# Attention steps in turns of two, in a fused two-layer kernel on one core

## The chip, the core and the metric

The kernel runs on one core of one Trainium2 chip. Its metric is the device time of one execution in microseconds, median of several. The engines are named as the profile names them: PE (TensorE matmul) with PEld (its weight loads), DVE (VectorE), ACT (ScalarE), POOL (GpSimd) and SP (SyncE, which here only issues transfers).

## What is computed

x has 8 sequences (batches) of 512 tokens and 256 channels, in float32. Two blocks follow each other, with 16 heads of 16 channels:

```python
x = x + _L0_attn_ref(_layernorm(x), Wqkv_w, Wqkv_b, conv_w, conv_b, out_w, out_b)
x = x + _L0_ffn_ref(_layernorm(x), wq, wk, wv, wo, w_router, wg, wu, wd, g1, g2)
```

The first: q, k, v; causal attention (a1); a convolution of three taps over its context, whose output is the q of a second causal attention (a2) on the same k and v; the output projection. The second: RMS norm, q and k rotated by position, causal attention (a3), output projection and residual; RMS norm, a router that picks 2 of 8 experts for each token, and the experts' gated units of 704. So there are three attentions for each of 8 batches.

## The kernel before, in words

`block_kernel` runs `fast_path`, and `general_path` after it only if counters at its end say so; with these inputs it doesn't run. All that follows is in `fast_path`.

**Attention.** `attention(qT, kT, v, to)` (L1100 on) is a generator for one of the 24 attentions. Keys are taken in blocks of 64 (NB = 8); a step takes one or two of them, so that each step has 512 columns of queries, and an attention has 9 steps (STEPS): four for the first 128 channels (`ch` 0), one that both halves share (the block `mid`), four for the second. A step does the following.

- Scores: on PE (L1188), 4 heads at a time in tiles of 32 rows, into two PSUM tiles `sc` of two banks each, for half of the heads each. The pool `ps_sc` has two buffers, so the next step writes the same two.
- Exponentials: on ACT (L1195), one for each half, from `sc` to the SBUF tile `pr` (four buffers).
- The mask of the diagonal blocks: on POOL (L1205).
- Values: `times_v` on PE (L1121) in tiles of 64 rows by 32 columns, into two banks `av`. It is put off: `behind` holds the functions of two steps, and `catch_up` runs the oldest.
- When a half's last block is in (`last`), `normalise` copies both `av` banks to `cs` on ACT (L1138), and SP moves their parts across partitions (`r<-cs`, then `cs<-cs`, L1146 and L1147). Two functions follow some steps later: `finish` on DVE (reciprocal and product in two halves, L1152 and L1153), and `check` on ACT (a sum for the counters, L1156).

**Units.** All other work of attention's stage is cut into units, which are methods of `Batch`:

- of a1: `stats`, `normed`, `transpose(d)`, `k(ch)`, `q(ch)`, `values(half)`
- between a1 and a2: `conv(ch, first, n)`, n of 6 terms of two channel halves and three taps; it keeps its bank until the last one
- between a2 and a3: `bias`, `x1(half)`, `stats2`, `transpose2(d)`, `k2(ch)`, `q2(ch)`, `values2(half)`, `normed2(c)`. `rotate` copies a projection on ACT, and its `rotation` follows on DVE; `split` then writes both halves of kT on ACT
- after a3: `h(half)`, `rms`, `transpose3(d)`, `route`, `slots`. `slots` puts eight transfers of rows to the experts' table into `to_send`, which `send` issues on POOL one by one.

Most units write a PSUM tile by `mm_tile`, which hands out two banks in turn, so a third unit needs the first one's bank emptied, by ACT or DVE.

**Order.** PE, ACT, DVE and POOL execute in the order in which the program emits (`manual_schedule`); SP isn't bound to it. Batches go in pairs, one in each lane. The order of attentions is a1 of both, a2 of both, a3 of both. Each step emits scores, values of the step two before, the mask, the functions due in `due[False]`, its units, those due in `due[True]`, and one `send`:

```python
                for step in range(STEPS):
                    next(steps)
                    next(steps)
                    next(steps)
                    follow_up(end=False)
                    beside(n, step)
                    follow_up()
                    send()
```

The units stand in tables by attention and step: `first_lane` and `second_lane` (a1's inputs of a coming batch), `between`, `middle` and `end`. Ahead of the first step stand all of batch 0's units, and batch 1's up to its transposes. `fill` writes a piece of the experts' table with padding by SP, one with each of the first 24 steps.

**Experts.** The last part (`expert_tile` and the loop over `places`) starts when attention ends; its first tile is begun among the last steps.

Of the kernel before, what the change touches and what calls it, by code (L numbers as in the profile page):

```python
# [18 lines left out]
P = 128  # L19
# [604 lines left out]
def fast_path(  # L624
# [28 lines left out]
    STEPS = DC * NB // 2 + 1  # L653

# [190 lines left out]
    with ExitStack() as att:  # L845
# [150 lines left out]
        def rotary_table(to, of):  # L996
            ps = mm_tile()
            for c in range(NC):
                t = small.tile([P, P], F32, tag="rope", name="rope", bufs=2)
                for a in range(2):  # L1000
                    nc.vector.tensor_copy(
                        t.rearrange("p (h a f) -> p h a f", a=2, f=HD // 2)[:, :, a],
                        of[a][:, c].unsqueeze(1).to_broadcast(halves),
                    )
                nc.tensor.transpose(ps[:, c * P : (c + 1) * P], t, ident)
            nc.scalar.copy(to, ps)

        def tables(n):
            if n == 0:
                nc.vector.tensor_scalar_mul(nsin_sb, sin_sb, -1.0)  # L1010
                rotary_table(cosT, (cos_sb, cos_sb))
            else:
                rotary_table(sinT, (nsin_sb, sin_sb))
# [74 lines left out]
        def catch_up():  # L1088
            for f in behind.pop(0):
                f()  # L1090


        due = {True: [], False: []}

        def follow(steps, f, end=True):
            due[end].append([steps, f])

        def follow_up(end=True):
            ready = [f for n, f in due[end] if n == 0]
            due[end][:] = [[n - 1, f] for n, f in due[end] if n]  # L1100
            for f in ready:
                f()

        def attention(qT, kT, v, to):

# [25 lines left out]
            def normalise(ch):  # L1131
# [26 lines left out]
                follow(2 - ch, finish)  # L1158
                follow(5 - 2 * ch, check, end=False)
# [21 lines left out]
            for parts in steps:  # L1181
# [14 lines left out]
                yield  # L1196
                if len(behind) == 2:
                    catch_up()
                behind.append([lambda parts=parts, pr=pr: values(parts, pr)])
                yield  # L1200
# [29 lines left out]
        class Batch:  # L1230
# [29 lines left out]
            def transposed(self, d, to, of, scale=None):  # L1260
# [5 lines left out]
                if scale is None:  # L1266
                    nc.scalar.copy(to[:, d, :S], ps)
                else:
# [149 lines left out]
            def transpose2(self, d):  # L1418
                if d == 0:
                    self.xaT = self.tile([P, DC, S], "xT", "xaT")  # L1420
                self.transposed(d, self.xaT, self.xa, g1_sb)

            def rotate(self, w, ch, to, later):
# [13 lines left out]
                follow(later - 1, rotation, end=False)  # L1437
                return t0

            def k2(self, ch, later=1):  # L1440
# [3 lines left out]
                t0 = self.rotate(wk_sb, ch, None, later)  # L1444
# [9 lines left out]
                follow(2 * later - 1, split)  # L1454

            def q2(self, ch, later=1):
                if ch == 0:
                    self.qT = self.q_tile("qT")
                self.rotate(wq_sb, ch, self.qT[:, ch, :], later)
# [123 lines left out]
        def first_lane(t):  # L1583

            return {
                (0, 4): [t.stats],
                (0, 6): [t.normed],
                (1, 0): [lambda: t.transpose(0)],
                (1, 1): [lambda: t.transpose(1)],
                (1, 2): [lambda: t.k(0)],  # L1590
                (1, 5): [lambda: t.q(0)],
                (2, 0): [lambda: t.values(0)],
                (2, 1): [lambda: t.values(1)],
                (2, 2): [lambda: t.k(1)],
                (2, 4): [lambda: t.q(1)],
            }

        def second_lane(t):

            return {  # L1600
                (0, 1): [t.stats],
                (0, 2): [t.normed],
                (0, 3): [lambda: t.transpose(0), lambda: t.transpose(1)],
                (1, 0): [lambda: t.k(0)],
                (1, 1): [lambda: t.q(0)],
                (1, 2): [lambda: t.values(0)],
                (1, 3): [lambda: t.values(1)],
                (1, 6): [lambda: t.k(1)],
                (2, 0): [lambda: t.q(1)],
            }  # L1610

        def conv_units(t, units):
            return {
                (0, step): [lambda ch=ch, first=first, n=n: t.conv(ch, first, n) for ch, first, n in fs]
                for step, fs in units.items()
            }

        def between(t):
            if t.lane == 0:
                units = {  # L1620
                    2: [(0, 0, 2)],
                    3: [(0, 2, 1), (1, 0, 1)],
                    4: [(1, 1, 2)],
                    5: [(0, 3, 2)],
                    6: [(0, 5, 1), (1, 3, 1)],
                    7: [(1, 4, 1)],
                    8: [(1, 5, 1)],
                }
            else:
                units = {  # L1630
                    1: [(0, 0, 2)],
                    3: [(0, 2, 2)],
                    4: [(0, 4, 2)],
                    5: [(1, 0, 1)],
                    6: [(1, 1, 2)],
                    7: [(1, 3, 2)],
                    8: [(1, 5, 1)],
                }
            units = conv_units(t, units)
# [52 lines left out]
        with tc.manual_schedule(  # L1692
# [8 lines left out]
            for fs in list(first.values())[2:]:  # L1701
                for f in fs:
                    f()
# [191 lines left out]
```

## Time and profile before

| | us |
|---|---|
| median of 3 runs | 1495.44 (1494.64 to 1496.28) |
| the profiled execution | 1502.59 |
| its span | 1500.7 |
| first scores to last values | 27.8 to 933 |
| first scores of pairs 0, 1, 2, 3 | 27.8, 256.8, 477.9, 700.7 |

The profiled execution's own time is 1.9 us over its span, and 7 us over the median of the runs. The profile is read by groups (a line of code, an engine, an operation), and by timelines, where a row has the start, the time, engine and line, tiles and shape, the number of instructions merged, and in brackets idle time before it with what ended it. A matmul in float32 stands in the trace as two passes, except transposes. Matmuls overlap and their ends are modelled, so what a burst of PE costs is read from its start to the next one's start.

### The profile page before, as it was taken

How to read it: one execution, taken by the hardware profiler on the slowest of the kernel's cores; microseconds unless marked ns; L12 is line 12 of the kernel's file. 1: busy time of each engine (PE TensorE's matmuls, PEld its weight loads, DVE VectorE, ACT ScalarE, POOL GpSimd, SP SyncE). 2: the span in 40 equal slices, each digit the busy share in tenths (PEclk: the TensorE clock that was granted, in tenths of full speed). 3: DMA queues.
4: the chain of work that ended last, by engine and by line, in shares of the span. 5: the costliest groups of instructions: out<-in, count | busy, mean ns of one | idle time of the engine just before them, and what ended most of it. 6: DMA issues, size and time to landing. Idle time of an engine off the chain costs nothing. (4 is left out here: it accounts for less than half of the span.)

```text
span 1500.7 us, 31797 instructions
## 1 busy us (share of the span) xinstructions
PE 1437.3 (96%) x13370; PEld 859.6 (57%) x13370; DVE 663.9 (44%) x1271; ACT 742.0 (49%) x1198; POOL 573.5 (38%) x615
## 2 busy tenths in 40 slices
PE   6799999999999999999999999999999999999995
PEld 3444555544555544555644545666676676676773
DVE  4153675663776653775643774422222222222221
ACT  3556788666788766788665885311112112112110
POOL 3333333563334563323563334443323323323322
PEclk9999999999999999999999998999999999999998
DMA  6920001210001210011211111242222313132300
GB/s 168 218 52 22 23 23 51 80 55 23 22 23 52 93 58 23 23 61 37 81 56 42 34 61 50 83 140 85 83 77 68 112 43 109 61 98 67 103 23 17
DMA packets 62841, 97.61 MB, mean 65 GB/s; under 512 B 13516, under 2 KB 39064, under 8 KB 62688
## 3 DMA queue, kind: packets, MB, share of 16 engines
q1 hardware_dynamic: 52608, 69.74, 15.6%
q0 software_dynamic: 10080, 25.74, 5.3%
q8 instruction: 107, 1.75, 0.5%
q14 instruction: 46, 0.38, 0.1%
HBM read 46.06 MB, written 32.61 MB: 52 GB/s over the span
## 5 line engine op out<-in xcount | busy, mean ns | idle before, releaser
L1195 ACT ACTIVATE pr<-sc 128x1024 f32<-128x1024 f32 x432 | 418.7, 1023 | 184.5 <-PE sc L1188 183.4
L1205 POOL TENSOR_TENSOR pr<-pr,seen 128x512 f32<-128x512 f32 (+1 forms) x216 | 249.6, 1156 | 461.2 <-ACT pr L1195 460.4
L761 PE MATMUL pgu<-xgT,gu 128*128 128x384 f32 x1056 | 347.7, 488 | 0.7 <-DVE hT L776 0.4
L761 PEld LDWEIGHTS pgu<-xgT,gu 128*128 128x128 f32 x1056 | 200.9, 191 | 136.1 <-issue 2.0
L775 ACT ACTIVATE sg<-pgu 128x384 f32<-128x384 f32 x120 | 58.9, 491 | 417.3 <-PE pgu L761 403.3
L1121 PE MATMUL av<-pr,va 64*32 64x512 f32 (+7 forms) x6144 | 244.5, 416 | 0.0
L1188 PE MATMUL sc<-qT,kT 32*128 32x512 f32 (+7 forms) x2048 | 187.6, 437 | 7.1 <-ACT pr L1195 6.3
L1152 DVE RECIPROCAL r<-r 128x256 f32<-128x256 f32 x96 | 167.6, 1746 | 59.0 <-DMA r<-cs 58.9
L785 PE MATMUL po<-dn,hT 128*128 128x256 f32 x864 | 190.9, 379 | 2.3 <-POOL hT L756 2.3
L802 POOL DMA_INDIRECT out_dram<-so_far,xg x72 | 72.3, 1004 | 290.5 <-DVE so_far L792 227.4
L785 PEld LDWEIGHTS po<-dn,hT 128*128 128x128 f32 x864 | 162.3, 190 | 24.2 <-POOL hT L756 2.7
L776 DVE TENSOR_TENSOR hT<-sg,pgu 128x384 f32<-128x384 f32 x120 | 66.4, 554 | 243.1 <-ACT sg L775 238.0
L1121 PEld LDWEIGHTS av<-pr,va 64*32 64x32 f32 x6144 | 94.1, 107 | 130.5 <-issue 86.9
L1188 PEld LDWEIGHTS sc<-qT,kT 32*128 32x128 f32 x2048 | 110.2, 185 | 97.4 <-issue 42.4
L1344 PE MATMUL mm<-cx,conv_sb 128*128 128x512 f32 x192 | 99.6, 634 | 11.1 <-DVE cx L1153 8.9
L792 DVE SCALAR_TENSOR_TENSOR so_far<-po,xg,so_far 128x256 f32<-128x256 f32 x72 | 34.8, 484 | 153.7 <-PE po L785 151.6
L747 POOL DMA_INDIRECT so_far<-out_dram,xg x72 | 74.1, 1029 | 54.1 <-issue 52.3
L1188 PE MATMUL sc<-q2T,kT 32*128 32x64 f32 (+7 forms) x1024 | 90.8, 434 | 0.3
L1563 POOL DMA_INDIRECT xtab<-rows,slot x64 | 65.3, 1020 | 54.6 <-DVE pick L1552 33.4
L1188 PEld LDWEIGHTS sc<-q2T,kT 32*128 32x128 f32 x1024 | 52.9, 184 | 52.9 <-issue 23.5
L1038 PE MATMUL mm<-xT,wqkv_sb 128*128 128x512 f32 x128 | 65.3, 636 | 0.0
L1038 PE MATMUL mm<-xaT,wqkv_sb 128*128 128x512 f32 x128 | 63.5, 618 | 0.0
(157 smaller groups left out, 1296.5 us busy)
## 6 DMA issues: line engine op xcount, KB each, us to landing
r<-cs SPq DMA_DIRECT2D x96, 128.0 KB
xtab<-pad SPq DMA_DIRECT2D x24, 397.5 KB
xg<-xtab SPq DMA_DIRECT2D x24, 397.5 KB
gu<-in_wg_dram SPq DMA_DIRECT2D x18, 352.0 KB
cs<-cs SPq DMA_DIRECT2D x48, 128.0 KB
gu<-in_wu_dram SPq DMA_DIRECT2D x18, 320.0 KB
dn<-in_wd_dram SPq DMA_DIRECT2D x9, 640.0 KB
out_dram<-x SPq DMA_DIRECT2D x9, 512.0 KB
```

The costliest lines, as they stand in the source:

```text
L747: nc.gpsimd.indirect_dma_start(out=so_far[:, s, :], out_offset=None, in_=out, in_offset=token_of(xg, s), bounds_check=B * S - 1, oob_is_er ...
L761: nc.tensor.matmul(ps, gu[d][:, n0 : n0 + P], xgT[:, d, :], start=(d == 0), stop=(d == DC - 1),)
L776: nc.vector.tensor_mul(hT[k], sg, pu)
L785: nc.tensor.matmul(po, hT[k][:, s * P : (s + 1) * P], dn[:, k, :], start=(k == 0), stop=(k == NK - 1),)
L802: nc.gpsimd.indirect_dma_start(out=out, out_offset=token_of(xg, s), in_=so_far[:, s, :], in_offset=None, bounds_check=B * S - 1, oob_is_er ...
L1038: nc.tensor.matmul(ps, w[:, d, n0 : n0 + P], srcT[:, d, :S], start=(d == 0), stop=(d == DC - 1),)
L1121: nc.tensor.matmul(av[i][g * HP : (g + 1) * HP, j * KB :], v[rows, j, ch * G + g, :], pr[rows, g, at : at + n], start=(j == 0), stop=(j == ...
L1152: nc.vector.reciprocal(r[:, half], r[:, half])
L1188: nc.tensor.matmul(sc[:, g - g0, at : at + S - j * KB], kT[r0 : r0 + HP, ch, j], qT[r0 : r0 + HP, ch, j * KB : S], start=True, stop=True,)
L1195: nc.scalar.activation(pr[:, g0 : g0 + 2], sc, AF.Exp, scale=SCALE)
L1205: nc.gpsimd.tensor_tensor(diag, diag, seen.unsqueeze(1).unsqueeze(1).to_broadcast([P, G, len(parts), KB]), ALU.mult,)
L1344: nc.tensor.matmul(ps, conv_sb[:, d, k, ch * P : (ch + 1) * P], self.cx[:, d, k : k + S], start=(t == 0), stop=(t == len(terms) - 1),)
```

## The change

It changes the order of the emission and leaves what is computed alone.

- The steps of all attentions form one sequence (`all_steps`), taken in turns of two; a pair of batches has 27 turns (TURNS). A turn emits the first step's scores, then `catch_up`, the mask, the functions due in `mid`, the second step's scores and mask, then all units of the turn in one stretch, those due in `end`, and two `send`.
- `attention` hands its values function out with a flag, `ends`, which says that a half's sums end with it. `catch_up` runs all that waits, up to and with one that ends.
- `finish`, `check`, `rotation` and `split` are put off by turns, and run at `mid` or `end`.
- One plan by turns takes the place of the five tables. `transpose2` empties its bank by DVE (`soon`), where it was ACT. The rotary tables are made in four parts.
- Ahead of the first step stand only batch 0's transposes, k(0) and q(0).

```diff
+    TURNS = 3 * STEPS
...
         def catch_up():
-            for f in behind.pop(0):
+            while behind:
+                f, ends = behind.pop(0)
                 f()
+                if ends:
+                    break
...
-        due = {True: [], False: []}
+        due = {"mid": [], "end": []}
...
-                follow(2 - ch, finish)
-                follow(5 - 2 * ch, check, end=False)
+                if ch == 0:
+                    follow(1, finish, "mid")
+                    follow(2, check, "mid")
+                else:
+                    follow(0, finish, "end")
+                    follow(1, check, "end")
...
-                yield
-                if len(behind) == 2:
-                    catch_up()
-                behind.append([lambda parts=parts, pr=pr: values(parts, pr)])
-                yield
+                ends = any(j == last[ch] and (ch, j) != (1, mid) for ch, j, _ in parts)
+                yield lambda parts=parts, pr=pr: values(parts, pr), ends
...
+                elif soon:
+                    nc.vector.tensor_scalar(
+                        to[:, d, :S], ps, scale[:, d : d + 1], None, ALU.mult
+                    )
...
-                follow(later - 1, rotation, end=False)
+                follow(0, rotation, "end")
...
-                follow(2 * later - 1, split)
+                follow(ch, split, ("mid", "end")[ch])
...
+            t = p * TURNS
+            plan(t, two, "q", 0)
+            plan(t, before0, "slots")
+            plan(t + 1, two, "values", 0, 1)
+            plan(t + 2, before1, "h", 0, 1)
+            plan(t + 2, before1, "rms")
+            plan(t + 3, two, "k", 1)
+            plan(t + 3, before1, "transpose3", 0, 1)
+            plan(t + 3, next0, "stats")
+            plan(t + 4, two, "q", 1)
+            plan(t + 4, before1, "route")
+            plan(t + 4, next0, "normed")
+            plan(t + 5, one, "conv", (0, 0, 3))
+            plan(t + 5, before1, "slots")
+            plan(t + 6, next0, "transpose", 0)
+            plan(t + 6, one, "conv", (0, 3, 3))
+            plan(t + 6, next0, "transpose", 1)
+            plan(t + 7, one, "conv", (1, 0, 4))
+            plan(t + 8, one, "conv", (1, 4, 2))
+            plan(t + 8, next0, "k", 0)
+            plan(t + 9, next0, "q", 0)
+            plan(t + 9, next0, "k", 1)
+            plan(t + 10, next0, "values", 0, 1)
             for c in range(NC):
+                plan(t + 10 + c, one, "bias", c)
+                plan(t + 14 + c, two, "bias", c)
+            plan(t + 11, two, "conv", (0, 0, 4))
+            plan(t + 12, two, "conv", (0, 4, 2), (1, 0, 2))
+            plan(t + 13, two, "conv", (1, 2, 2))
+            plan(t + 14, two, "conv", (1, 4, 2))
+            plan(t + 15, one, "x1", 0, 1)
+            plan(t + 15, one, "stats2")
+            plan(t + 16, next0, "q", 1)
+            plan(t + 16, one, "transpose2", 0, 1)
+            plan(t + 16, one, "k2", 0)
+            plan(t + 16, one, "q2", 0)
+            plan(t + 17, one, "q2", 1)
+            plan(t + 17, one, "k2", 1)
+            plan(t + 18, one, "values2", 0, 1)
+            plan(t + 19, two, "x1", 0, 1)
+            plan(t + 19, two, "stats2")
+            plan(t + 20, two, "transpose2", 0, 1)
+            plan(t + 20, two, "k2", 0)
+            plan(t + 21, two, "q2", 0)
+            plan(t + 21, two, "k2", 1)
+            plan(t + 21, next1, "stats")
+            plan(t + 22, two, "values2", 0)
+            plan(t + 22, two, "q2", 1)
+            plan(t + 22, next1, "normed")
+            plan(t + 23, two, "values2", 1)
+            plan(t + 23, next1, "transpose", 0, 1)
+            for c in range(NC):
+                plan(t + 19 + c, one, "normed2", c)
+                plan(t + 25 + c // 2, two, "normed2", c)
+            plan(t + 24, one, "h", 0, 1)
+            plan(t + 24, one, "rms")
+            plan(t + 25, one, "transpose3", 0, 1)
+            plan(t + 26, one, "route")
+            plan(t + 26, next1, "k", 0)
...
+            for n in range(n_turns):
+                for half in range(2):
+                    step = next(steps)
+                    if half == 0:
+                        catch_up()
+                    behind.append(step)
                     next(steps)
-                    next(steps)
-                    next(steps)
-                    follow_up(end=False)
-                    beside(n, step)
-                    follow_up()
-                    send()
+                    if half == 0:
+                        follow_up("mid")
+                for f in units.pop(n, ()):
+                    f()
+                follow_up("end")
+                send()
+                send()
```

Here `one` and `two` are the pair's batches, `before0` and `before1` the pair's before it, `next0` and `next1` those of the next. In the first five turns other plans stand: batch 0's values, k(1) and q(1) and batch 1's transposes in turn 0, the rest of batch 1's a1 units in turns 1 to 4, the rotary tables in turns 2 to 7, and two `fill` with each of the first twelve turns.

## The prediction

> **What bounds the kernel now.** I read the page's engine shares first, then its costly groups, then PE's timeline in attention.
>
> ```profile
> span 1500.7 us, 31797 instructions
> ...
> PE 1437.3 (96%) x13370; PEld 859.6 (57%) x13370; DVE 663.9 (44%) x1271; ACT 742.0 (49%) x1198; POOL 573.5 (38%) x615
> ...
> L1195 ACT ACTIVATE pr<-sc 128x1024 f32<-128x1024 f32 x432 | 418.7, 1023 | 184.5 <-PE sc L1188 183.4
> ```
>
> PE is called busy 96% of the time, and everything else about half. So PE sets the pace; but the 96% hides time lost between bursts, and only start-to-start times show it:
>
> ```profile
> 135.19 1.17 PE L1188 MATMUL sc<-q2T,kT 32*128 32x384 f32 x16
> 136.29 1.52 PE L1121 MATMUL av<-pr,va 64*32 64x512 f32 x32
> 137.74 1.98 PE L1344 MATMUL mm<-cx,conv_sb 128*128 128x512 f32 x4
> 139.65 1.17 PE L1188 MATMUL sc<-q2T,kT 32*128 32x320 f32 x16
> 140.75 1.09 PE L1121 MATMUL av<-pr,va 64*32 64x448 f32 x32
> 141.77 1.12 PE L1344 MATMUL mm<-cx,conv_sb 128*128 128x512 f32 x2
> 142.83 1.20 PE L1188 MATMUL sc<-q2T,kT 32*128 32x512 f32 x8
> ```
>
> These are two steps: scores (L1188), values (L1121), a unit (here conv). Four conv passes take 1.91 (137.74 to 139.65), two take 1.06: a pass of 512 columns costs 0.425, and a unit's burst 0.21 beside its passes. A score burst has two passes' worth (0.85) and takes 1.10: 0.25 beside. A value burst takes 1.02 for 0.85, and 1.45 for 1.28: 0.17 beside. That is the price of changing between the three tile shapes.
>
> Next, how long the exponentials hold the score banks, from one burst and ACT's rows for it:
>
> ```profile
> 383.39 1.17 PE L1188 MATMUL sc<-q2T,kT 32*128 32x256 f32 x16
> ```
> ```profile
> 384.65 1.94 ACT L1195 ACTIVATE pr<-sc 128x1024 f32<-128x1024 f32 x2 [3.64 <-PE sc L1188]
> ```
>
> With ACT idle, the first exponential starts 1.26 after the burst, and both are done 3.20 after it. The score tiles have two buffers, one for each half of a step, so no score burst can finish its second half before that: its end is max(PE ready, 3.20)+1.10. The kernel before shows this where little lies between two score bursts:
>
> ```profile
> 243.82 1.22 PE L1188 MATMUL sc<-qT,kT 32*128 32x448 f32 x16
> 244.97 0.66 PE L1121 MATMUL av<-pr,va 64*32 64x256 f32 x16
> 246.72 2.31 PE L1188 MATMUL sc<-qT,kT 32*128 32x384 f32 x16 [1.09 <-ACT pr L1195]
> 248.95 2.81 PE L1121 MATMUL av<-pr,va 64*32 64x512 f32 x32
> ```
> ```profile
> 244.90:248.40 3.50, 2.41 (x36) 1.37 (x32) 1.48 (x5) 3.47 (x9) 2.67 (x3) 1.00 0.44 150
> 248.40:251.80 3.40, 3.40 (x39) 1.10 (x36) 0.84 (x1) 2.17 (x4) 1.78 (x2) 0.50 0.40 84
> ```
>
> Only a 0.6 value burst stands between; PE waits 1.09, the second score burst takes 2.23 instead of 1.10, and then the granted clock (seventh number of the windows) is 0.50 for 3.4 us: the next value burst takes 2.75 instead of 1.45.
>
> **The change, part by part.** A turn is: scores (S1), values of two earlier steps (V), scores (S2), all units (U). T0 to T26 are the 27 turns of a pair of batches; there are four pairs.
>
> *Bursts removed.* The two instruction orders give, from the first score to the last value, 216 score, 216 value and 200 unit bursts before; 213, 108 and 108 after. At 0.25, 0.17 and 0.21: 54+37+42=133 before, 53+18+23=94 after. **-38 us.** No row shows S to U or V to S as the usual passage; at 0.17 for all removed it is -34, at 0.25 -50.
>
> *Waits of the old order.* A middle pair takes 222.8 (first scores at 477.89 and 700.72). Work in it: 54 steps at 1.10+1.02=114.5; units 87.3, namely 16 q/k projections, 8 value halves and 8 output halves at 4 passes (1.71 each, 54.6), 24 conv terms of 0.85 (20.5), 12 transposes of 0.64 (7.7), two routes of 1.75, two slots of 0.45; 50 bursts at 0.21 (10.5). Sum 212, so about 10 per pair is waiting, and the old places of it go: **-40 us.** As the sum of small differences it is 6 to 14 per pair (-24 to -56).
>
> *The floor under S2.* Now only V separates S1 from S2. V starts at 1.10; S2 could start after V's passes and 0.17. A step's values are 0.85, but the middle step splits into 0.43 at once and 0.43 with step 5, and catch_up stops where a half's sums end. So nine turns have V passes of 1.71, 1.71, 0.43, 2.99, 0.85, 2.56, 1.28, 2.13, 1.71. Against 3.20 the waits are 0.22, 0.22, 1.50, 0, 1.08, 0, 0.65, 0, 0.22: 3.9 per nine turns, twelve times: **+47 us.** It needs nothing but an idle ACT; a busy one adds.
>
> *ACT leftovers and banks.* Formerly values and a unit (some 3 us) lay between what ACT had left over and the next scores. Now whatever ACT has queued at the end of U delays S1's exponentials, so S2, so all units. By ACT's new order and its rows (0.57 per context copy or check, 0.62 per copy of values, 1.34 for both halves of split, 0.97 per exponential): in T18, U ends at 4.33+0.21+3.42=7.96; ACT is at 3.20+1.14+0.57+1.94=6.85, then copies of values2 to 8.1 and 9.3, split to 10.7. T19's exponentials could start at 7.96+1.26=9.2: 1.4 late. In T20, transpose2 needs xa, whose chain in the trace ends 6.4 after x1 leaves PE (383.39 to 389.8); S1, V, S2 cover 4.5: 1.9 late. In T23, exponentials 1.1 late (values copy, t copy, normed2, split), and the second transpose wants the bank of values2, one of two, whose copy waits behind both exponentials: 1.0. Likewise T25 1.5 (squares and check of T24; a U of only 1.3), T26 0.9, T3 1.7 (squares, third bank), T6 1.1 (the second half of cx: finish stands behind slots on DVE), T14 and T16 0.5 each, others 0.4. Sum 12 per pair: **+48 us.** Bounds: 0 if each leftover fits into the 1.26 before the first exponential; 24 per pair if all are double. A gain is excluded, since the floor is already what an idle ACT gives. I take 12, as each item is a sum of rows.
>
> *Clock.* T3, T12 and T21 repeat the place above (S, 0.43 of values, S). It occurs four times in the old trace and dropped the clock twice; a drop costs 3.4/2=1.7. Longer waits stand in five more turns. Against the few drops of the old attention I take two more, **+3 us**, from 0 to 16 more (+27). The Trainium skill, "TensorE: Matmul & The Clock Gate", section "Why this matters for your kernels", asks only for no idle gap over about 3 us. By it none of my waits would cost clock and this term is 0; the trace disagrees, with 1.09 of idleness before a drop.
>
> The skill's "TensorEngine Tiling", "PSUM Bottleneck", speaks against the whole change: tiling speeds up matmuls, not the emptying of PSUM. The rows are 1.10 for scores against 1.94 for their exponentials; taken as a throughput limit it gives 4 x 0.97=3.9 per turn of 8.2, no cost at all, so it bites only through the floor.
>
> *Moved and free.* Values, k and q of batch 0 and the transposes of batch 1 (some 9 us of PE) go from ahead of the first scores into T0. This buys nothing: the first conv waits to 74.97 for cx, that is for the r copies, which stand behind 17 fills on SP in both orders (DVE waited 26.3 for them). The second r landed at 82.3, cx by 87; the new order wants it some 4 us earlier: **+4 us.** xaT goes from ACT to DVE (16 of 0.69 against 0.75 for a like row), the rotary tables into four parts: in the terms above, or once and under a microsecond. Fills and sends stay two per two steps; POOL's mask of S2 is done by 3.23+3.20+1.3=7.7, its values are multiplied 1.1+0.85 into the next turn, near 10: covered by U; without U it would cost up to 1.
>
> **Sum:** -38-40+47+48+3+4=+24. The profiled execution (span 1500.7, 1502.6 in all) would become 1527; on the median 1495.4 it is **1519**.
>
> **Rivals.** *Faster* (0.29): the leftovers vanish because ACT, 49% busy, has room, and PE gains what the bursts cost. -38-40+47+4=-27, 1468; with a quarter of the leftovers 1480. For it: xaT leaves ACT, half finishes and splits sit where DVE is free. Against: the same two exponentials that must precede S2 stand behind them in ACT's order. It decides if leftovers and clock stay under 27 us (7 per pair).
>
> *No change* (0.08): leftovers of about 6 per pair, 1495.
>
> *Much slower* (0.15, part of my forecast): each wait above 1.3 drops the clock as often as in the old trace, half of 8 per pair: +27 instead of +3, 1543. For it: two drops in four. Against: half-rate PE also lets ACT catch up.
>
> *It doesn't merge*: excluded, the order has 436 passages for 632.
>
> **How the numbers follow.** Slower 0.63, its own range 1503 to 1548; faster 0.29; within 0.2% (3 us, about what this kernel's runs can tell apart) 0.08. The range reaches down to 1474, most of the faster case, and up to 1548.
>
> **What would show it.** Right: PE's idle time before L1200 released by ACT's pr grows from some 7 to over 40 us; the S1-to-S2 distance is 3.2 or more nearly everywhere; more stretches at 0.5; a pair takes about 226. Wrong on leftovers: S2 starts at 3.2 in T19, T23, T25 as well. Wrong on bursts: S to U costs less than 0.2. If V holds its 0.17 but a pair falls under 218, the rival is right.

## The result, and the profile after

The changed kernel takes 1550.27 us (median of 4 runs, 1543.94 to 1555.88) where the kernel before takes 1495.08 (1494.64 to 1496.28). The ratio is 1.0367, with a 95% interval of 1.0321 to 1.0412: slower, as forecast, by 55 us where 24 were forecast, and 2 us outside the range. The profiled execution took 1555.88, its span 1553.8.

These are lines of the page of the changed kernel: engine shares, then groups, each with its busy time, the mean of one in ns, and the idle time ahead of it with what ended it.

```profile
span 1553.8 us, 31746 instructions
...
PE 1454.9 (94%) x13370; PEld 918.9 (59%) x13370; DVE 669.1 (43%) x1287; ACT 730.7 (47%) x1184; POOL 577.6 (37%) x615
...
L1207 ACT ACTIVATE pr<-sc 128x1024 f32<-128x1024 f32 x432 | 419.2, 1026 | 209.5 <-PE sc L1200 181.9
...
L1200 PE MATMUL sc<-qT,kT 32*128 32x64 f32 (+7 forms) x2048 | 208.0, 440 | 25.0 <-ACT pr L1207 21.2
...
L1357 PE MATMUL mm<-cx,conv_sb 128*128 128x512 f32 x192 | 98.2, 650 | 10.4 <-DVE cx L1161 10.4
...
L1200 PE MATMUL sc<-q2T,kT 32*128 32x128 f32 (+7 forms) x1024 | 102.7, 434 | 5.2 <-ACT pr L1207 5.2
```

The exponentials themselves are as before (419 us). PE's idle time before scores that exponentials ended is 21.2+5.2=26.4 us, against 6.3 in the kernel before:

```profile
L1188 PE MATMUL sc<-qT,kT 32*128 32x512 f32 (+7 forms) x2048 | 187.6, 437 | 7.1 <-ACT pr L1195 6.3
```

PE still looks 94% busy, so again the bursts have to be read from start to start. Each distance from one burst to the next was taken apart for this: its columns at full rate (two tiles of 64 columns side by side count once, a transpose as 0.16) with the prediction's burst prices; half of the time at half clock, as far as the distance is longer than that; the rest, called waits. The zero of the waits is arbitrary (small matmuls cost more than their columns), so only their changes are read:

| us, profiled executions | predicted | before | after | change |
|---|---|---|---|---|
| bursts, at 0.25, 0.17, 0.21 | -38 | | | -38.2 |
| work moved into the stretch (columns) | +9 | | | +10.6 |
| waits | -40+47+48+4=+59 | 68.3 | 131.2 | +62.9 |
| half clock | +3 | 16.4 | 30.5 | +14.1 |
| first scores to last values | | 905.4 | 954.7 | +49.3 |
| ahead of the first scores | -9 | 27.8 | 20.7 | -7.1 |
| from the last values to the end | 0 | 567.6 | 578.4 | +10.8 |
| span | +24 | 1500.7 | 1553.8 | +53.1 |

These are single executions, and the runs of the changed kernel spread over 12 us, so differences of a few us between traces say little. Of the waits, those before or inside scores went from 29.0 to 79.7 us, those of units from 31.6 to 42.5, those of values from 7.7 to 9.0. Pairs took 239.3, 238.0 and 239.5 (before: 229.0, 221.1, 222.8).

**The floor.** T12 of pair 2, a turn in which ACT had nothing left over, on PE's timeline of the changed kernel (start, time, engine and line, tiles, shape, instructions, idle time before):

```profile
605.26 1.22 PE L1200 MATMUL sc<-q2T,kT 32*128 32x448 f32 x16
606.41 0.66 PE L1129 MATMUL av<-pr,va 64*32 64x256 f32 x16
607.65 2.06 PE L1200 MATMUL sc<-q2T,kT 32*128 32x384 f32 x16 [0.57 <-ACT pr L1207]
609.63 2.84 PE L1357 MATMUL mm<-cx,conv_sb 128*128 128x512 f32 x6
```

From S1 to the unit it takes 4.37. Bursts alone would take 1.10+0.43+0.17+1.10=2.80; the prediction's floor is 3.20+1.10=4.30. S2 starts 2.39 after S1 already, into the score tile that the first exponential has emptied, and is then drawn out to 1.98, since its second half needs the second tile. So most of this wait counts as busy PE. The other undisturbed turns agree: 4.32 in T1, 4.38 in T5, T14 and T21, 4.35 in T7 (means of pairs 1 to 3).

**Leftovers.** T23 of the same pair:

```profile
701.91 1.22 PE L1200 MATMUL sc<-qT,kT 32*128 32x448 f32 x16
703.06 1.09 PE L1129 MATMUL av<-pr,va 64*32 64x320 f32 x32
705.34 2.05 PE L1200 MATMUL sc<-qT,kT 32*128 32x384 f32 x16 [1.19 <-ACT pr L1207]
707.33 3.34 PE L1061 MATMUL mm<-wqkv_sb,xaT 128*64 128x128 f32 x32
```

Here S1 to U takes 5.42: 1.1 more than the floor, which is what the prediction gave T23's late exponentials.

**The largest wait in a pair** is in T6, for the second half of cx. First PE, then DVE, then the window that follows (busy time of the five engines with counts, and the granted clock):

```profile
554.98 1.17 PE L1200 MATMUL sc<-qT,kT 32*128 32x256 f32 x16
556.08 0.66 PE L1272 MATMUL mm<-ident,xn 128*128 128x128 f32 x4
559.95 4.54 PE L1357 MATMUL mm<-cx,conv_sb 128*128 128x512 f32 x6 [3.22 <-DVE cx L1161]
```
```profile
553.96 0.17 DVE L1567 CAST slot<-red 128x4 int32<-128x4 f32 x1
554.04 1.75 DVE L1160 RECIPROCAL r<-r 128x256 f32<-128x256 f32 x1
555.88 1.89 DVE L1161 TENSOR_TENSOR cx<-cs,r 128x256 f32<-128x256 f32 x1
557.70 1.74 DVE L1160 RECIPROCAL r<-r 128x256 f32<-128x256 f32 x1
559.47 0.43 DVE L1161 TENSOR_TENSOR cx<-cs,r 128x256 f32<-128x256 f32 x1
```
```profile
561.00:564.40 3.40, 3.40 (x6) 1.23 (x5) 0.00 (x0) 0.00 (x0) 0.97 (x1) 0.51 0.22 80
```

finish starts in the same breath in which slots ends (554.04), with no wait of its own: by the trace its copies had landed by 551.85, and it stood in DVE's queue behind route and slots. Then one product takes 1.89 instead of 0.43, PE waits 3.22, and with the wait come 3.4 us of half clock, in which six conv passes take 4.33 instead of 2.56.

**A slow product also makes T2's wait**, 1.5 beyond the floor in pairs 1 to 3. DVE's product at the end of T1, then ACT:

```profile
510.46 3.18 DVE L1161 TENSOR_TENSOR c<-cs,r 128x256 f32<-128x256 f32 x1
515.39 0.63 ACT L1164 ACTIVATE cs<-r 128x512 f32<-128x512 f32 x1 [3.72 <-issue]
516.02 1.92 ACT L1207 ACTIVATE pr<-sc 128x1024 f32<-128x1024 f32 x2
```

check (515.39) needs the second half of r, which DVE makes behind that product, and it stands ahead of the exponentials in ACT's queue. T2's first scores start at 513.24, so the exponentials could have started at 513.24+1.26=514.50, 1.5 earlier.

**The passage into the experts**, which the prediction took to be unchanged:

```profile
984.93 2.32 PE L786 MATMUL po<-dn,hT 128*128 128x256 f32 x10
992.54 1.19 PE L786 MATMUL po<-dn,hT 128*128 128x256 f32 x2 [5.29 <-issue]
993.53 5.76 PE L1032 MATMUL mm<-wo_sb,c 128*128 128x256 f32 x16
999.13 5.34 PE L786 MATMUL po<-dn,hT 128*128 128x256 f32 x24
1008.29 2.03 PE L1272 MATMUL mm<-ident,rows 128*128 128x128 f32 x8 [3.82 <-DVE rows L1502]
```

The two last passes of an output need the last piece of hT, which DVE does at 991.88, behind slots and finish. The 3.82 at 1008 are the chain of rms: DVE's scaling of ss took 3.24 us beside POOL's work where it took 0.35 before, and the power that follows stood behind an addition and a transfer in POOL's queue. Half clock goes with both waits (991.0 to 997.9, 1008.1 to 1011.5).

### The profile page after: what moved, and what is told of

Same layout as the page of the kernel before. It is cut to its first block, busy times and chain, and to the rows that moved or that the text cites. A ratio compares the mean times of both kernels' runs of the same rounds, so it can differ in the third digit from the quotient of the medians.

```text
span 1553.8 us, 31746 instructions
## 1 busy us (share of the span) xinstructions
PE 1454.9 (94%) x13370; PEld 918.9 (59%) x13370; DVE 669.1 (43%) x1287; ACT 730.7 (47%) x1184; POOL 577.6 (37%) x615
## 5 line engine op out<-in xcount | busy, mean ns | idle before, releaser
L1214 POOL TENSOR_TENSOR pr<-pr,seen 128x512 f32<-128x512 f32 (+1 forms) x216 | 253.7, 1177 | 506.5 <-ACT pr L1207 505.2
L1200 PE MATMUL sc<-qT,kT 32*128 32x64 f32 (+7 forms) x2048 | 208.0, 440 | 25.0 <-ACT pr L1207 21.2
L1129 PE MATMUL av<-pr,va 64*32 64x512 f32 (+7 forms) x6144 | 218.5, 410 | 0.0
L1200 PEld LDWEIGHTS sc<-qT,kT 32*128 32x128 f32 x2048 | 124.6, 186 | 106.8 <-ACT pr L1207 40.1
L1129 PEld LDWEIGHTS av<-pr,va 64*32 64x32 f32 x6144 | 113.9, 106 | 101.8 <-issue 72.9
L1200 PE MATMUL sc<-q2T,kT 32*128 32x128 f32 (+7 forms) x1024 | 102.7, 434 | 5.2 <-ACT pr L1207 5.2
L1200 PEld LDWEIGHTS sc<-q2T,kT 32*128 32x128 f32 x1024 | 63.0, 184 | 51.1 <-issue 21.8
L1357 PEld LDWEIGHTS mm<-cx,conv_sb 128*128 128x128 f32 x192 | 36.3, 203 | 54.5 <-issue 41.6
L1365 DVE TENSOR_SCALAR q2T<-mm,convb_sb 128x512 f32<-128x512 f32 x16 | 12.0, 751 | 130.0 <-PE mm L1357 130.0
```

The lines of the kernel that those rows point to most:

```text
L1129: nc.tensor.matmul(av[i][g * HP : (g + 1) * HP, j * KB :], v[rows, j, ch * G + g, :], pr[rows, g, at : at + n], start=(j == 0), stop=(j == ...
L1200: nc.tensor.matmul(sc[:, g - g0, at : at + S - j * KB], kT[r0 : r0 + HP, ch, j], qT[r0 : r0 + HP, ch, j * KB : S], start=True, stop=True,)
L1214: nc.gpsimd.tensor_tensor(diag, diag, seen.unsqueeze(1).unsqueeze(1).to_broadcast([P, G, len(parts), KB]), ALU.mult,)
L1357: nc.tensor.matmul(ps, conv_sb[:, d, k, ch * P : (ch + 1) * P], self.cx[:, d, k : k + S], start=(t == 0), stop=(t == len(terms) - 1),)
```

## Experiments

Every ratio is to the kernel before, run on the same chip, where its median was between 1496.8 and 1499.6. "First to last" is first scores to last values.

**Is it the order or the plan?** Three kernels. `by_steps` takes the new plan in the old order; a turn's units are cut in two by their cost:

```diff
+                first_half, second_half = split(n)
                 for half in range(2):
                     step = next(steps)
-                    if half == 0:
-                        catch_up()
+                    if len(behind) == 2:
+                        behind.pop(0)[0]()
                     behind.append(step)
                     next(steps)
                     if half == 0:
                         follow_up("mid")
-                for f in units.pop(n, ()):
-                    f()
+                    for f in (first_half, second_half)[half]:
+                        f()
```

> The new plan of units in the old order: each step emits scores, the values of the step two before it, and half of its turn's units. Theory (the order of a turn is at fault: only values stand between its two score bursts, so the second waits for exponentials and for what ACT still holds): the bursts come back (+38 us against the changed kernel) but the waits of scores for exponentials, some 70 us with the clock they cost, mostly go: 1500 to 1520 us. Rival (the new places of the units are at fault, by DVE and bank waits): the time stays at 1550 or rises to 1590 by the bursts.

Measured: 1599.39, 1.0657 (1.0632 to 1.0682), 102 us of half clock between first and last. That is above both ranges, and the theory as it was put then (the new order makes the loss, so the new plan is harmless in the old one) missed. But the run doesn't test the plan's quality. In it the first half of a turn's units comes before the second scores, half a turn earlier than planned, and the values of a turn's last step come behind the next turn's second scores, half a turn later. Units meet data that isn't there:

```profile
582.91 5.49 PE L1357 MATMUL mm<-cx,conv_sb 128*128 128x512 f32 x6 [5.64 <-DVE cx L1161]
...
709.85 1.73 PE L1272 MATMUL mm<-ident,xa 128*128 128x128 f32 x8 [3.32 <-DVE xa L1408]
```

These two are T6 and T20, in the old order with the new plan: the places of the units suit one order only. The waits of units are 79.8 us here, those at scores 35.2, little over the 29.0 of the kernel before.

`units_split` keeps the new order of values and puts the first half of the units between V and S2 (`catch_up()` as in the changed kernel, units as in the diff above).

> As the changed kernel, with values of two steps in one burst, but about half of a turn's units stand between the values and the second scores. Theory (order of a turn): it keeps the saving of value bursts alone (108 at 0.17, 18 us against the kernel before) and its waits are about those of the kernel before plus the few that the data of the new plan cause: 1480 to 1505 us. Rival (places of units): above 1530 us.

Measured: 1581.85, 1.0534 (1.0506 to 1.0563). The trace shows why the theory missed: in a middle pair the waits in S2 fall from 13 to 2 us, but those in S1 rise from 2 to 10. With half of the units gone from behind S2, the next S1 comes too soon for the same exponentials.

`order_alone` is the opposite: the old tables and the old ways of putting off, with scores and values in the new order.

```diff
-                (1, 1): [lambda: t.values2(0)],
-                (1, 2): [lambda: t.values2(1)],
+                (1, 1): [lambda: t.values2(0), lambda: t.values2(1)],
...
-                follow(later - 1, rotation, end=False)
+                follow(later - 1, rotation)
...
+            for two in range(0, len(order_of) * STEPS, 2):
+                for half in range(2):
+                    step = next(steps)
+                    if half == 0:
+                        catch_up()
+                    behind.append(step)
+                    next(steps)
+                for half in range(2):
+                    follow_up(end=False)
+                    beside(*divmod(two + half, STEPS))
+                    follow_up()
+                    send()
```

> The old tables of units and the old way of putting functions off, in the new order: S1, V, S2, then the units of both steps. Two edits beside it: values2(1) stands one step earlier and a rotation follows its own unit at once, as the new order needs them there. Bursts fall by about 38 us as in the changed kernel. Theory A, the order itself costs the time (second scores wait for the exponentials with only values between, +50 or so, and the waits drop the clock): 1505 to 1530 where the kernel before takes 1495 to 1500. Theory B, the new places of the units make the loss and the order is a gain: below 1490. Theory C, the new plan was needed to make the order bearable: 1540 and more.

Measured: 1568.38, 1.0476 (1.0432 to 1.0520); the bursts and columns fell by 41 us, waits rose by 81 and half clock by 19. Of the waits, 43 came at scores, 31 at units and 7 at values. The time is that of C: in the new order the new plan is worth some 16 us (1.0476 against 1.0367). With by_steps this makes a square: either half of the change alone is slower than both together, so order and plan have no price of their own each. But the waits at scores come with the order, under both plans, and hardly at all with the plan alone. Waits of units with the old tables, in T5 and at the start of T18:

```profile
569.91 3.78 PE L1344 MATMUL mm<-cx,conv_sb 128*128 128x512 f32 x4 [3.62 <-DVE qT L1321]
...
677.51 1.14 PE L1191 MATMUL sc<-qT,kT 32*128 32x512 f32 x8 [2.93 <-DVE qT L1435]
```

Both wait for a q that DVE writes. The projection behind the second runs in the same stretch, directly ahead of the scores that need it (from 670.87). The rest was not taken apart.

**The exponentials.** `half_exp_after` and `half_exp_before` shorten each exponential:

```diff
-                    nc.scalar.activation(pr[:, g0 : g0 + 2], sc, AF.Exp, scale=SCALE)
+                    nc.scalar.activation(
+                        pr[:, g0 : g0 + 2, : S // 2], sc[:, :, : S // 2], AF.Exp, scale=SCALE
+                    )
```

> The changed kernel, with exponentials of the first 256 of the 512 columns alone (the others keep values written before), so each pair of them takes 1.1 us where it took 1.94; scores, values and units are all there. Theory (the second scores wait for exponentials): the floor of 12 us per pair falls to 3, leftovers of ACT by half, and the clock drops with them: 1460 to 1490 us. Rival (PE's own work or DVE and banks set the loss): above 1525 us.

> The kernel before with each exponential on the first 256 of its 512 columns only; the exponentials of the other columns are left out, and those columns of pr keep what was written earlier. The mate of half_exp_after, which took some 8 us off the changed kernel. If the old order pays little for its exponentials (page: 6.3 us of PE idle before scores released by ACT, some more inside score bursts): 1488 to 1498, so that the two gain about alike. If short exponentials are worth more to the new order, as the floor under S2 says, this one gains less than 4 us and the changed kernel's remaining waits are others. A gain of over 20 us would say that the exponentials set the old order's pace too.

Measured: the changed kernel 1543.56 (2 runs), 1.0288 (1.0257 to 1.0320), some 12 us less than 1.0367 gives at that median, 4 to 20 by the intervals; the kernel before 1495.62, 0.9974 (0.9962 to 0.9986), 4 us less. The first lies with its rival (above 1525), far from the theory. The medians understate both, as the edit also fills four tiles of pr on POOL at the start (7.2 us), and the first scores come 4.8 and 4.6 us later. From first scores to last values, short exponentials take 17 us off the changed kernel and 10 off the kernel before. In the changed kernel the waits at scores fall from 79.7 to 29.6 us, but those of units and values rise from 51.5 to 81.0, and half clock by 3.5. The largest rise is in T6: in the two middle pairs PE's wait for cx grew from 3.2 us to 4.3 and 5.9, and the half clock with it from 3.4 to 6.8.

**DVE's queue and the passage.** `slots_later` moves slots from T0 to T1 and from T5 to T7, and check by one turn:

```diff
-            plan(t, before0, "slots")
+            plan(t + 1, before0, "slots")
-            plan(t + 5, before1, "slots")
+            plan(t + 7, before1, "slots")
-                    follow(2, check, "mid")
+                    follow(3, check, "mid")
-                    follow(1, check, "end")
+                    follow(2, check, "end")
```

> The changed kernel with slots one turn (before0) and two turns (before1) later, and check one turn later. Theory (finish stands behind route and slots on DVE, which keeps conv of turn 6 waiting 3.2 us and then drops the clock, and check behind finish keeps ACT from turn 2's exponentials): turn 6 falls from 13.9 to about 9, turn 2 from 9.5 to 8; about 6.5 us per pair, 1520 to 1530 us. Rival (turn 6 waits for the r copies themselves): 1545 to 1555 us.

Measured: 1551.68, 1.0331 (1.0297 to 1.0365), which the interval of the changed kernel doesn't tell from no gain. The time is the rival's, its reason isn't: T6's wait for cx fell from 3.2 to 1.3 us, so it was the queue. But the value bursts took 3 us more per pair.

`tile_first_after` changes the passage alone:

```diff
-            go_on(first_tile, 3)
-            batches[B - 2].slots()
+            go_on(first_tile, 4)
             follow_up("end")
+            batches[B - 2].slots()
...
             t.h(1)
-            go_on(first_tile)
             t.rms()
```

> The changed kernel; after the last attention the first expert tile's last piece of hT and one more output pass stand ahead of finish and of slots, in place of behind them. Theory: PE's wait of 5.29 at 987 and the half clock after it (3.4 us, 1.7 lost) go: 4 to 7 us under the changed kernel, 1543 to 1548. Rival: h then waits for finish as long as the pass did, within 2 us of the changed kernel. In the attentions nothing changes.

Measured: 1563.00, 1.0420 (1.0402 to 1.0439): worse. The wait of 5.29 is gone, and a larger one has come:

```profile
991.25 3.69 PE L1032 MATMUL mm<-wo_sb,c 128*128 128x256 f32 x16
994.98 2.86 PE L786 MATMUL po<-dn,hT 128*128 128x256 f32 x12
1014.62 2.02 PE L1272 MATMUL mm<-ident,rows 128*128 128x128 f32 x8 [16.78 <-DVE rows L1502]
```

slots is later, so its eight sends fill POOL's queue just as rms wants its power from POOL.

`slots_and_sends` draws both lessons: slots of T5 to T7, check where it was, and in the passage the sends behind rms.

```diff
-            plan(t + 5, before1, "slots")
+            plan(t + 7, before1, "slots")
...
-            batches[B - 2].slots()
             follow_up("end")
             go_on(first_tile)
-            sends(4)
+            batches[B - 2].slots()
             go_on(first_tile)
-            sends(4)
...
             t.rms()
+            sends(8)
```

> The changed kernel; slots of T5 at T7, so that finish on DVE no longer stands behind route and slots; and behind the last attention the eight sends are put behind rms, and finish and the last piece of hT ahead of slots. Theory of the waits of T6 (3.2 and 1.7 of half clock in a pair): 8 to 14 us less from the first score to the last value, 950 to 960 for 954.7. Theory of the passage into the experts (DVE's order, then POOL's queue of sends ahead of the power in rms): 7 to 12 us less from the last value to the end, 566 to 572 for 578.4. Both: 1527 to 1542. Rival for the second: waits move on by the queue again, as in the run before that put the tile first: 578 or more.

Measured: 1535.06, 1.0252 (1.0221 to 1.0283), 17 us less than the changed kernel. First to last it is 942.7 for 954.7, and from there to the end 568.7 for 578.4: 12 and 9.7 us less, where the theories had 8 to 14 and 7 to 12 (the "950 to 960" beside the first doesn't fit its own 8 to 14). Of the 12, 8.7 are half clock. In the passage PE's two waits are 2.15 and 1.00 us now. T6 has no wait any more:

```profile
544.49 1.17 PE L1200 MATMUL sc<-qT,kT 32*128 32x256 f32 x16
545.59 0.66 PE L1272 MATMUL mm<-ident,xn 128*128 128x128 f32 x4
546.08 2.74 PE L1357 MATMUL mm<-cx,conv_sb 128*128 128x512 f32 x6
```

**Filling the short turns.** `short_filled` puts one unit between V and S2 in five turns of a pair:

```diff
+            return turn > 5 and place in (
+                (3, "k", (1,)),
+                (5, "conv", (0, 0, 3)),
+                (12, "conv", (0, 4, 2)),
+                (21, "q2", (0,)),
+                (23, "values2", (1,)),
+            )
...
                     if half == 0:
                         follow_up("mid")
+                        for f in filling.pop(n, ()):
+                            f()
```

> The changed kernel; in the turns T3, T5, T12, T21 and T23 of every pair, where values of only 0.43 or 0.85 us separate the two score bursts, one unit of the turn (k(1), three conv terms, two conv terms, q2(0), values2(1)) is put between V and S2, as two more burst passages each. Theory (the floor under S2, of any work short between the two score bursts): per pair 2.0+1.1+1.5+1.5+2.1=8.3 of waits before and in S2 go, 2 of bursts come back, and some half-clock time goes; 16 to 35 us in all under the changed kernel: 1515 to 1537. Rival (the exponentials then hold up the next turn's first scores, since fewer units are left between S2 and S1): within 5 us of the changed kernel's 1545 to 1555.

Measured: 1550.23, 1.0356 (1.0332 to 1.0381): the rival. T23 and the turn after it:

```profile
693.49 1.97 PE L1061 MATMUL mm<-wqkv_sb,xaT 128*64 128x128 f32 x32
695.39 1.42 PE L1200 MATMUL sc<-qT,kT 32*128 32x384 f32 x16
696.73 0.66 PE L1272 MATMUL mm<-ident,xn 128*128 128x128 f32 x4
698.52 0.66 PE L1272 MATMUL mm<-ident,xn 128*128 128x128 f32 x4 [1.13 <-ACT va L1075]
699.57 2.97 PE L1200 MATMUL sc<-qT,kT 32*128 32x320 f32 x16 [0.39 <-ACT pr L1207]
```

S2 no longer waits (695.39, in 1.34), but the second transpose and the next S1 do, 1.13 and 0.39, and that S1 is drawn out to 2.90.

`all_three` puts the two edits before together.

> Both of the edits before in one kernel. If the terms add up: 1500 to 1525, the kernel before or slightly over it. If what one frees the other takes (the score banks' turn sets the pace whichever unit stands where): no more than 5 us under the better of the two.

Measured: 1539.73, 1.0287 (1.0242 to 1.0332), no better than slots_and_sends.

**What the floor is worth without the queue.** `half_exp_slots_sends` is slots_and_sends with the short exponentials.

> slots_and_sends with each exponential on the first 256 of its 512 columns only; the exponentials of the other columns are left out, and those columns of pr keep what was written earlier. In half_exp_after the shorter exponentials took 9.5 us per middle pair off the waits at the score bursts, and 5 of it came back as longer waits of units for cx and xa and as half clock. Theory (the floor under S2 is real, and was hidden there by the queue of slots and finish): without that queue short exponentials are worth 20 to 40 us: 1497 to 1517 where slots_and_sends took 1535. Rival (the units' chains hold the turns' lengths whatever the scores do): 1523 and more.

Measured: 1512.49, 1.0094 (1.0072 to 1.0115): 24 us under slots_and_sends at the same median, inside the theory's 20 to 40, where the kernel before gains 4. First to last it is 915.7 for 942.7, 27 us less, against 10 in the kernel before. So the exponentials cost the new order some 17 us more than the old. The edit shortens what ACT has left over as well, so this is the floor and the leftovers together. That the queue on DVE had hidden it isn't shown: T6's loss grows by 2.4 us per middle pair here and by 2.6 in half_exp_after; what differs is that there the waits of values rose by 13 us, and here they didn't. What still stands over the kernel before, first to last, is 16 us more of units that wait, 13 of values and 7 of half clock, beside the work moved in, against 38 of bursts saved. T20 as an example:

```profile
660.50 1.14 PE L1205 MATMUL sc<-qT,kT 32*128 32x512 f32 x8
662.97 0.65 PE L1279 MATMUL mm<-ident,xa 128*128 128x128 f32 x2 [1.33 <-DVE xa L1415]
664.03 1.33 PE L1279 MATMUL mm<-ident,xa 128*128 128x128 f32 x6 [0.40 <-DVE xa L1415]
665.52 3.27 PE L1048 MATMUL mm<-xaT,wqkv_sb 128*128 128x512 f32 x4 [0.17 <-DVE xaT L1285]
```

**The r copies.** The first conv of pair 0 waits 7.95 us in the kernel before, as SP's rows in its profile show: the first r copies, issued at 57.21, stand behind 17 fills, and cs, which needs them, is issued at 70.00.

```profile
48.04 9.07 SPq L916 DMA_DIRECT2D xtab<-pad  x4
57.21 1.66 SPq L1146 DMA_DIRECT2D r<-cs  x2
58.92 2.16 SPq L916 DMA_DIRECT2D xtab<-pad  x2
70.00 0.47 SPq L1147 DMA_DIRECT2D cs<-cs  x1
```

`fills_spread_before` emits one fill at every second step:

```diff
-                plan(n // STEPS, {(0, n % STEPS): [lambda n=n: fill(n)]})
+                plan(2 * n // STEPS, {(0, 2 * n % STEPS): [lambda n=n: fill(n)]})
```

> The kernel before with one fill of the experts' table at every second step instead of every step. Theory: the first r copies stand behind 9 fills instead of 17, land some 10 us earlier, and the first conv no longer waits 7.95 us with 10 us of half clock about it: 1482 to 1491. Rival: the next units or the second r copies take the wait over, within 3 us of the kernel before (1495 to 1500).

Measured: 1499.55, 0.9995 (0.9978 to 1.0011), no change, and for a plain reason: in its trace the same 17 fills stand ahead. SP isn't bound to the emission, and a fill depends on nothing. `fills_paced_before` gives it something to depend on, a write of POOL ahead of each:

```diff
             to = xtab.rearrange("(p r) w -> p r w", p=P)[:, n * per : (n + 1) * per]
+            nc.gpsimd.memset(pad[:, :1], 0.0)
             written.append(
```

> The kernel before, with POOL writing one column of the padding anew ahead of each fill, so that the fills can't all be issued by SP at the start; spacing the emission alone left 17 of them ahead of the first r copies. Theory: with some 8 fills ahead of them, done by then, the first r lands near 60 for 70, PE's wait of 7.95 for cx and some 5 of its half clock go: 1484 to 1493 for 1499. Rival: the scores' exponentials or the second r copies hold pair 0 to the same time, within 3 us.

```profile
35.69 18.12 SPq L917 DMA_DIRECT2D xtab<-pad  x6
53.90 1.20 SPq L1147 DMA_DIRECT2D r<-cs  x2
58.82 0.47 SPq L1148 DMA_DIRECT2D cs<-cs  x1
```

Measured: 1494.09, 0.9976 (0.9959 to 0.9993), 1 to 6 us under the kernel before by the interval: a little faster than both kernels, but between the theory (6 to 15) and its rival (within 3), so it proves neither. The first copies now take 5 us instead of 13, and the first conv doesn't wait. But fills that wait for POOL hold up the copies behind them, since SP keeps their order, and a later conv still waits 1.67.

`slots_sends_fills` has the same edit in slots_and_sends.

> slots_and_sends with the paced fills of fills_paced_before. Theory: in pair 0 the first conv no longer waits for r copies behind 17 fills; 4 to 10 us under slots_and_sends, 1525 to 1531. Rival: within 3 us, since in turns the first scores, 7 us earlier, meet the loads of the weights in any case.

Measured: 1540.04, 1.0278 (1.0243 to 1.0314), no gain: there no conv of the first turns waited for cx without the edit, and with it the second burst of conv waits 2.89.

## Why the prediction was right or wrong

*Direction, and the reason for it:* right. The waits at scores rose by 51 us in the changed kernel and by 43 in order_alone, but by 6 in by_steps, which has the new plan without the order; short exponentials take 50 of them away again in the changed kernel.

*Bursts, -38:* -38.2 by count, but at the prediction's own price, which no run tests. (The "436 passages" among the rivals are 429 by its own counts; nothing rests on it.)

*Waits of the old order, the floor, the leftovers and the r copies (-40+47+48+4=59):* 63 together. The floor alone is right to 0.1 us in the turns where ACT is idle. Of the leftovers T23 (1.1), T19 (1.4 for 1.5) and T20 (1.9 for 2.1) were right, and T6 was the one that was much too small: 1.1 for 3.2 and a drop of the clock. The prediction saw that finish stands behind slots there, but not that route stands ahead of both, nor that a product can take 1.89. T2 (1.5 beyond the floor) wasn't in the list, nor T9 and T10 of the last pair, which have no units left (PE idles 1.68 and 1.19 behind their scores). The 4 of the r copies came as a wait of 3.93 in T5 of the first pair, but for a piece of the rotary tables, whose copies stand on DVE behind finish. The single terms can't be told apart further, as the old waits went with the old order.

*Clock, +3:* 14 between first and last. The step that failed is "I take two more": there were 15 stretches of half clock there, 61.4 us, against 6 of 34.1 us before, which is eight more drops of 3.4. It also looked in the wrong turns: none of the eight waits in T12 and T21 (0.57 each) brought half clock, while T6 brought it in all of pairs 1 to 3, T3 in two of these and T23 in two pairs of four. The upper end, +27, was about as far off on the other side. The rival that it made, 1543, came nearest to the time, though its mechanism gives only half of its 27.

*The sum's own gap:* it had no term for what follows the last attention. Its edits were in the diff (parts of the first tile pulled into the last turns, finish and slots in another order), and they cost 10.8 in spite of 2.5 us of work less, which had moved into the attentions; slots_and_sends took 9.7 of it back. At 13 together this is the largest single miss, with the clock's 11 next. At the start, 8.1 us of work moved away and the first scores came 7.1 earlier, 1 less.

So 31 us were missing between forecast and result. The profiled executions differ by 53 where 24 were forecast, 29 more: the passage with its moved work 13, the clock 11, the waits 4, the start 1.

*The signs to look for:* the idle time before scores was to grow to over 40; it grew to 26, because a score burst that waits in its middle counts as busy. S1 to S2 was to be 3.2 or more; it is less in 52 of 108 turns, down to 2.39 (2.28 in the very first, which has no values), because S2 starts into the first score tile: the floor holds S2's end, as the formula had it, not its start. In T19, T23 and T25, where a start at 3.2 was to show the leftovers wrong, S2 starts 3.9, 3.4 and 3.5 after S1. A pair was to take 226 and took 238 to 240. The rival "faster" is out: a pair under 218 was its mark.

*Open:* what half_exp_slots_sends still takes over half_exp_before (1.0094 to 0.9974, some 18 us) was not taken apart by a run. By the traces, first to last, it has 21 us more of waits at scores, 15 at values and 10 of half clock, against the bursts saved.

## What to carry to other kernels

Where two bursts of one kind share a pair of PSUM tiles, the work between them must be as long as the engine that empties the tiles takes; lumping other work elsewhere saves its passages and pays that floor, and pushing work back between them moves the wait to the next pair. An order of units and the places of their inputs belong together: a new order needs its in-order queues walked through again one by one (here DVE's route, slots, finish, and POOL's sends ahead of a small operation). The same holds where a loop ends and the next stage starts: each line that the diff moves there needs a term.

## What the hardware showed beside this

A product of two SBUF tiles on DVE (finish's) took 0.42 to 0.43 us in all of the 61 cases in which no POOL tensor operation ran beside it, and up to 3.27 in the other 35. Of the 26 slow ones, 20 end 0.28 or 0.29 us after the POOL operation does. The page "SBUF — State Buffer" of the Trainium skill, section "SBUF: two separate sides", says that an operation with two SBUF inputs and one of GpSimd that reads SBUF lock each other out for their whole length. The product of 555.88 fits this, as it ended at 557.77:

```profile
556.20 1.29 POOL L1214 TENSOR_TENSOR pr<-pr,seen 128x512 f32<-128x512 f32 x1
```

By the page the one that starts first goes first; by the rows the product started 0.32 us ahead of the mask and still came behind it, so that part isn't borne out here.

The clock fell to half after waits far under 3 us: of the 17 stretches of half clock between the first scores and 1015 us in the changed kernel, seven follow a wait of 3.2 us or more, nine one of 0.65 to 2.31, and one no wait over 0.3. No length of wait decides it alone: 1.19 in T23 brought half clock in two pairs of four. The rule of "TensorE: Matmul & The Clock Gate" that the prediction weighed, "Why this matters for your kernels", covers the seven only.
